# Norms, logits and choice of experts of a routed FFN, made block by block inside the attention stream before it

## The chip, the cores and the metric

The kernel runs on one core of one Trainium2 chip. The metric is the device time of the whole kernel in microseconds (us): the median over runs, lower is better. The time before is 7800.91 us, the median of three runs (7788.05 to 7835.12).

The engines are named as in the profile: PE is TensorE (PEld its weight loads), DVE is VectorE, ACT is ScalarE, POOL is GpSimd, SP is SyncE, which here only issues DMAs. Each runs its own queue in order, and semaphores tie the queues together.

## The reference, cut to what matters

Four layers run over 6250 nodes of 256 numbers. Every edge list has 206,250 edges, in order of their target node. The change touches the first two layers:

```python
x = x + _L0_gnn_ref(_layernorm(x), edge_index, ...)      # attention over the edges
x = x + _L0_ffn_ref(_layernorm(x)[None], ...)[0]         # routed FFN, 8 experts, top 2
x = x + _L1_gnn_ref(_layernorm(x), src, dst, edge_weight, ...)
x = x + _L1_ffn_ref(_layernorm(x)[None], ...)[0]

def _L0_ffn_ref(x, Wr, br, ln_g, ln_b, W1, b1, W2, b2):  # N = 6250, D = 256, E = 8, H = 1024
    xt = x.reshape(N, D)
    logits = xt @ Wr + br
    probs = softmax(logits)
    top_p, top_idx = top_k(probs, 2)
    weights = top_p / top_p.sum(-1, keepdims=True)
    xn = (xt - mean(xt)) * rsqrt(var(xt) + 1e-5)
    xe = xn[None] * ln_g[:, None] + ln_b[:, None]        # for each expert
    h = gelu(xe @ W1 + b1);  y = h @ W2 + b2
    return (weights[:, :, None] * y at top_idx).sum(1)
```

So the FFN's input is normed once (xt, which the router reads) and once more without weights (xn, which the experts read).

## The kernel before, in words

X, the nodes' state, stays in SBUF as 49 blocks of 128 nodes. The inputs are sorted on the chip in other places of the program; here the path `fast()` runs, which the kernel takes when the edges are in order of their targets.

**The first attention's stream** (`gat_stream`, called for `s0`). First come the edge rows (L1792 on), then the projection (L1809 to 1838), which writes one row of 260 numbers for each node to a table in DRAM (`tab`) and keeps each node's two parts of the score in `NI`. `gat_stream` splits these into three bfloat16 parts, `NB` (L1170 to 1175), and stores them to DRAM (L1177); `NB` lies in a pool that lives as long as the stream.

The edges are cut into 1612 tiles of 128 and 202 pieces of 8 tiles. For each tile, POOL gathers 128 rows of `tab` with an indirect DMA (L1214) into one of nine buffers `g`. Four pieces make a batch (51 of them). The order of the work on each engine is written out by hand (`manual_schedule`): one step of the loop issues the gathers of piece s, loads for piece s+2 on SP's queue (`db`, the targets, L1198; `nbw`, the nodes' parts, L1203; `kf`, L1207), the scores of piece s-2 (`z`, L1246, from `g` and one-hot matmuls), moves of finished sums, and the sums of piece s-7 (L1316). Once in four steps, a batch turns its scores (L1260), takes the greatest of each node by scans, turns them back, and ACT takes exponentials (L1281, L1285); DVE scales the gathered rows into messages (L1293). When the last tile of a group of nodes is summed, ACT copies the sum (`kept`, L1329, three buffers), PE shifts it into blocks (`bacc`, L1342), and `done` (L1845 to 1861) ends block b: it divides by the softmax's sum, adds the bias, takes the relu and adds to X (L1861). At the end of each part of a step `beside()` is called, which here does nothing.

**The routed FFN's head** (`ffn0`, L652 to 690) follows. For seven blocks at a time, `layernorm` (L247 to 257: statistics L252 and L253, a root on ACT at L242, a reciprocal L244, a subtract-and-scale L256) gives `xt` and, from it, `xn`. SP stores `xn` to the DRAM table `tab_x` (L671). Each block of `xt` is transposed on PE (L263), copied by ACT (L264), multiplied with Wr (L678), and DVE adds br into `lo` (L679). Then for all 49 blocks at once come softmax, `top2` (each of 392 numbers ranked against the 7 others of its node: L270 to L278), and the weights of the two chosen (`gates`, L290).

**The experts** (`routed_ffn`, L457 to 632). It loads b1, ln_g and ln_b with the biases along the partitions (L481, three DMAs, then DVE copies at L482 and a store to `par_d` at L483). The routing counts each expert's nodes with scans (L486), gives every choice a place (L491 to L538), and turns places into row numbers with 98 pairs of one-hots and a matmul (L549, L551, L553). Then 56 tiles of 256 rows: SP loads the expert's weights, POOL gathers the rows from `tab_x` (L577), PE turns them (L586), DVE scales them into `xe` (L589), and PE makes two matmul layers (L601, L614) with ACT's Gelu between (L604); POOL scatters the result (L617). After each tile four pieces of other work are issued from a generator, `beside`.

That other work is a sort of the second edge list (`sorted_edges`, L1405 on; its compares at L1447 and L1448 on DVE), then the preparation of the later streams' runs. The generator's work carries no dependence on the FFN's head. Outside the stream a scheduler orders the instructions, and it puts the sort's first operations into DVE's queue from the end of the stream on.

After that come the second GNN layer (POOL gathers at L234, weighted sums at L1921) and a second attention stream whose gathers are again at L1214.

Of the kernel before, what the change touches and what calls it, by code (L numbers as in the profile page):

```python
# [20 lines left out]
F32 = mybir.dt.float32  # L21
BF = mybir.dt.bfloat16
I32 = mybir.dt.int32
I16 = mybir.dt.int16
AF = mybir.ActivationFunctionType
# [7 lines left out]
P = 128  # L33
# [38 lines left out]
def tile_kernel(ctx, tc, src_ins, out):  # L72
# [192 lines left out]

    def top2(pool, v, n_exp, nt=NT):
# [3 lines left out]
        nc.vector.memset(rank, 0.0)  # L270
        for j in range(n_exp):
            for a, b, op in ((0, j, OP.is_gt), (j + 1, n_exp, OP.is_ge)):
                if a < b:
                    nc.vector.tensor_tensor(cmp[:, :, a:b], v[:, :, j:j + 1].to_broadcast([P, nt, b - a]),
                                            v[:, :, a:b], op=op)
                    nc.vector.tensor_add(rank[:, :, a:b], rank[:, :, a:b], cmp[:, :, a:b])
# [4 lines left out]
    def per_row(pool, op, a, n_exp, name):  # L281
        r = pool.tile([P, NT], F32, name=name)
        nc.vector.tensor_reduce(r, a, AX.X, op)
        return r[:, :, None].to_broadcast([P, NT, n_exp])

    def divide(pool, dst, a, by, n_exp, name):
        r = pool.tile([P, NT], F32, name=name)
        nc.vector.tensor_reduce(r, by, AX.X, OP.add)
        nc.vector.reciprocal(r, r)
        nc.vector.tensor_mul(dst, a, r[:, :, None].to_broadcast([P, NT, n_exp]))  # L290
# [166 lines left out]
    def routed_ffn(keep, tab_x, sel, gates, pre, beside):  # L457
# [12 lines left out]
        par_d = dram.tile([n_exp, P, NPAR], F32, name="par_d")  # L470
# [4 lines left out]
        with tc.tile_pool(name="rk", bufs=1) as p, tc.tile_pool(name="rkw", bufs=4) as wp, \  # L475
                tc.tile_pool(name="rk_ps", bufs=1, space=PSUM) as pp:
            par = p.tile([P, n_exp, NPAR], F32, name="par")
            with nc.allow_non_contiguous_dma(reason="biases along the partitions"):
                for o, n, v in ((0, FC, b1), (FC, KD, I[f"{pre}_ln_g"]), (FC + KD, KD, I[f"{pre}_ln_b"])):
                    pt = p.tile([P, n_exp, n], F32, name=f"par{o}")  # L480
                    nc.sync.dma_start(pt, v.rearrange("e (c p) -> p e c", p=P))  # L481
                    nc.vector.tensor_copy(par[:, :, o:o + n], pt)  # L482
                nc.sync.dma_start(par_d.rearrange("e p c -> p e c"), par)  # L483
# [168 lines left out]
    def ffn0(beside):  # L652

        E0 = I["L0_ffn_Wr"].shape[1]
        with tc.tile_pool(name="f0", bufs=1) as f0:
            gates = f0.tile([P, NT, E0], F32, name="gates")
# [1461 lines left out]
```

## Time and profile before

| | us |
|---|---|
| median of three runs | 7800.91 (7788.05 to 7835.12) |
| the profiled execution's own time | 6605.39 |
| its span | 6603.6 |
| first gather of the first stream | 173.8 |
| last gather of the first stream ends | 2206.7 |
| last block of X is written | 2251.1 |
| `gates` are written | 2396.6 |
| first one-hot of the routing | 2418.2 |
| first matmul of the experts | 2476.3 |
| experts end | about 3324 |

Busy in the whole span: PE 3864.8, PEld 2941.4, DVE 4398.8, ACT 1008.9, POOL 4097.0 us. The profiled execution is one run, 1195 us shorter than the median of the timed runs; the profile's page doesn't say why. The mean granted TensorE clock of that execution is 0.75.

How to read the profile's lines: a group gives source line, engine, operation, out<-in with the tiles' names and shapes, the count, then the busy time in us, the mean of one in ns, and the idle time of the engine just before, with what ended most of it. A line of the timeline gives start and length in us and, in brackets, the idle time before and what released it; "SPq" is a DMA issued by SP. A line of the waits gives the engine, what it was about to do, whom it waited for, and us in total, times and the longest. In the page's 40 slices (165 us each) POOL is busy 7 tenths in slices 2 to 13 and 2 to 3 tenths in slices 14 to 20; PE is at 9 tenths in slices 16 to 19:

```profile
PE   4466666666666659999913566666666667111111
DVE  5455555555555683345267888888888883888888
ACT  2000000000000102222300122222222223000000
POOL 0777777777777302233217777777777775777774
```

### The profile page before, as it was taken

Reading aid. Unit: us, or ns where it says so; the run is one execution under the profiler, and the core shown is the slowest. Engines: PE = TensorE matmul, PEld = TensorE weight load, DVE = VectorE, ACT = ScalarE, POOL = GpSimd, SP = SyncE. Lnnn points to the kernel's source line nnn. Section 1 sums busy time; section 2 is a strip of 40 time slices with the busy share of each in tenths; the row PEclk is TensorE's granted clock in tenths of the full one; section 3 lists DMA queues with packets and bytes.
Section 4 is the critical chain, followed back from the end, with each engine's and each line's share of the span. In section 5 each row is a group of like instructions: output and inputs, shape, how many; then the busy total and the mean of one; then the engine's idle time right before and its main releaser. Section 6 shows DMA issues by size and latency. Waiting matters only on the chain.

```text
span 6603.6 us, 62175 instructions
## 1 busy us (share of the span) xinstructions
PE 3864.8 (59%) x17463; PEld 2941.4 (45%) x17463; DVE 4398.8 (67%) x10540; ACT 1008.9 (15%) x2527; POOL 4097.0 (62%) x4320
## 2 busy tenths in 40 slices
PE   4466666666666659999913566666666667111111
PEld 3344444444444448888712344444444445111111
DVE  5455555555555683345267888888888883888888
ACT  2000000000000102222300122222222223000000
POOL 0777777777777302233217777777777775777774
PEclk9677777777777669999955777787888788555555
DMA  4544454554555216556553444444444443222322
GB/s 134 140 139 137 138 140 138 138 139 137 138 139 138 72 45 210 184 191 218 181 188 107 115 118 123 122 122 118 123 122 122 118 122 75 61 68 69 68 68 53
DMA packets 495558, 821.80 MB, mean 124 GB/s; under 512 B 142672, under 2 KB 314915, under 8 KB 495170
## 3 DMA queue, kind: packets, MB, share of 16 engines
q0 software_dynamic: 190880, 462.26, 26.3%
q1 hardware_dynamic: 291654, 343.79, 17.0%
q10 hardware_dynamic: 12668, 11.68, 0.6%
q8 instruction: 141, 2.31, 0.1%
q14 instruction: 215, 1.76, 0.1%
HBM read 743.27 MB, written 77.29 MB: 124 GB/s over the span
## 4 chain that ended last, share of the span: by engine, by line
POOL 33%; PE 17%; issue 17%; DVE 16%; DMA 16%; ACT 1%; DVEq 0%; ACTq 0%; SPq 0%; another core or an unknown queue 0%; POOLq 0%
POOL g L234 17%; POOL g L1214 16%; DMA g<-tab,si 7%; PE ph L601 5%; PE py L614 5%; DMA g<-tab_ef,si 3%; PE acc L1316 3%; DMA g<-tab_1f,si1s 2%; DVE run L1921 2%; DVE X L1756 2%; DVE g L1293 1%; DVE oh L1107 1%; PE ph L1830 1%; DVE ot L1224 1%; DVE z L1246 1%
## 5 line engine op out<-in xcount | busy, mean ns | idle before, releaser
L234 POOL DMA_INDIRECT g<-tab_ef,si x1616 | 1533.1, 949 | 601.7 <-issue 574.3
L1214 POOL DMA_INDIRECT g<-tab,si x1612 | 1539.6, 955 | 493.7 <-issue 411.2
L1921 DVE SCALAR_TENSOR_TENSOR run<-g,wab,run 128x256 f32<-128x256 f32 x2626 | 1264.5, 488 | 337.7 <-DMA g<-tab_ef,si 261.3
L1316 PE MATMUL acc<-g,oh 128*128 128x264 f32 x3224 | 1054.0, 493 | 338.4 <-DVE g L1293 333.4
L1316 PEld LDWEIGHTS acc<-g,oh 128*128 128x128 f32 x3224 | 780.7, 250 | 561.7 <-DVE g L1293 392.0
L1214 POOL DMA_INDIRECT g<-tab_1f,si1s x787 | 770.1, 979 | 251.5 <-issue 212.5
L2035 PE MATMUL acc<-run,oh 128*128 128x256 f32 x808 | 320.8, 537 | 707.7 <-DVE oh L1925 707.0
L2035 PEld LDWEIGHTS acc<-run,oh 128*128 128x128 f32 x808 | 199.6, 264 | 817.6 <-issue 431.2
L1246 DVE TENSOR_TENSOR z<-g,nd 128x32 f32<-128x32 f32 (+1 forms) x301 | 58.1, 193 | 717.5 <-DMA g<-tab,si 654.8
L1293 DVE TENSOR_TENSOR g<-g,pe 128x2048 f32<-128x2048 f32 (+2 forms) x301 | 487.4, 1619 | 0.0
L1657 PE MATMUL pf<-xt,w 128*128 128x512 f32 (+1 forms) x832 | 419.0, 639 | 105.9 <-ACT h L1662 99.1
L1316 PE MATMUL acc<-s,oh 128*128 128x72 bf16 x1267 | 96.7, 251 | 593.6 <-DVE s L1298 593.6
L1668 PE MATMUL pf<-w,h 128*128 128x256 f32 x1568 | 400.2, 405 | 68.2 <-ACT y L1673 56.9
L601 PE MATMUL ph<-xe,w 128*128 128x256 f32 x1792 | 404.1, 382 | 4.3 <-DVE xe L589 4.3
L614 PE MATMUL py<-w,h 128*128 128x256 f32 x1792 | 398.6, 380 | 0.0
L577 POOL DMA_INDIRECT xg<-tab_x,gi x112 | 123.7, 1105 | 403.6 <-PE pt L586 317.9
L1668 PEld LDWEIGHTS pf<-w,h 128*128 128x128 f32 x1568 | 314.3, 205 | 128.6 <-ACT y L1673 64.5
L601 PEld LDWEIGHTS ph<-xe,w 128*128 128x128 f32 x1792 | 340.9, 192 | 49.8 <-DVE xe L589 4.7
L1316 PEld LDWEIGHTS <-oh 128*128 128x128 bf16 x1267 | 90.4, 134 | 597.5 <-issue 494.1
L614 PEld LDWEIGHTS py<-w,h 128*128 128x128 f32 x1792 | 336.5, 191 | 42.9
L617 POOL DMA_INDIRECT tab_y<-y,so x112 | 119.0, 1063 | 275.3 <-DVE y L616 270.8
L1235 PEld LDWEIGHTS <-ot 128*128 128x128 bf16 x2879 | 116.1, 101 | 388.2 <-DVE ot L1224 347.2
(494 smaller groups left out, 5764.0 us busy)
## 6 DMA issues: line engine op xcount, KB each, us to landing
w<-in_L_ffn_W SPq DMA_DIRECT2D x112, 1024.0 KB
db<-s_d SPq DMA_DIRECT2D x299, 256.0 KB
g<-tab_ef,si POOLq DMA_INDIRECT x1616
g<-tab,si POOLq DMA_INDIRECT x1612
y_d<-y SPq DMA_DIRECT2D x196, 128.0 KB
yb<-y_d SPq DMA_DIRECT2D x49, 512.0 KB
g<-tab_1f,si1s POOLq DMA_INDIRECT x787
yy<-tab_y SPq DMA_DIRECT2D x7, 1792.0 KB
```

The costliest lines, as they stand in the source:

```text
L234: nc.gpsimd.indirect_dma_start(out=dst, out_offset=None, in_=table, in_offset=bass.IndirectOffsetOnAxis(ap=si[:, t:t + 1], axis=0))
L601: nc.tensor.matmul(ph, w1[:, k, f * P:(f + 1) * P], xe[:, k, :], start=(k == 0), stop=(k == KD - 1))
L614: nc.tensor.matmul(py, hs[f][:, i * P:(i + 1) * P], w2[:, f, :], start=(f == 0), stop=(f == FC - 1))
L1214: nc.gpsimd.indirect_dma_start(out=g[:, j, :DH + H], out_offset=None, in_=tab, in_offset=bass.IndirectOffsetOnAxis(ap=si[:, t0 + j:t0 + j ...
L1246: nc.vector.tensor_add(z[:, :n], g[:, :n, DH:DH + H], nd[:, :n, :H])
L1293: nc.vector.tensor_mul(gh, gh, ps[i][:, o:o + n, :, None].to_broadcast([P, n, H, CD]))
L1316: nc.tensor.matmul(acc[b].rearrange("p s w -> p (s w)"), oh[:, t - a], m_, start=(t == lo), stop=(t == hi))
L1657: nc.tensor.matmul(ph[:, :n], w1[:, e, k, f * P:(f + 1) * P], xts[g][:, k, :n], start=(k == 0), stop=(k == KD - 1))
L1668: nc.tensor.matmul(py[:, :D], hs[g, e, f][:, j * P:(j + 1) * P], w2[:, e, f, :], start=(f == 0), stop=(f == FC - 1))
L1756: nc.vector.scalar_tensor_tensor(X[:, b, :], v[:, e, :], gates[:, j, e:e + 1], X[:, b, :], op0=OP.mult, op1=OP.add)
L1921: nc.vector.scalar_tensor_tensor(at[:, i] if j < Q - 1 else r[i], g[:, j, :], w, at[:, i], op0=OP.mult, op1=OP.add)
L2035: nc.tensor.matmul(acc[i], oh[:, k], r[k], start=(q % 2 == 0 and k == 0), stop=(last and k == 1))
```

## The change

The head of the FFN moves into the stream. A class `Head` holds `lo`, `sel`, `gates`, `wr`, `br` and the two DRAM tables; it is made before the edge rows are loaded, so the loads of `wr` and `br` stand first on SP's queue. The bias loads become a generator (`expert_params`), of which a step runs at each `beside()` of the stream: the three loads at its first step, the copies and the store 20 steps later.

Every ending of a block now goes on over the following steps of the stream, one part in each: `done` returns `normed`, that returns `twice`, that `logits`. Each adds statistics and a root of one block (`spread`) or a reciprocal and a scaling (`scaled`); `twice` makes the transposes, `logits` writes the block's row to `tab_x` (49 stores of 128 KB where there were seven of seven blocks) and the logits, which ACT copies from PSUM. After blocks 21, 43 and 48 the choice of experts is made for the blocks since the last choice (22, 22 and 5), one part in each step (`select`, `ranks`).

Around it: the exponentials `pe`, the transposes and the logits share one PSUM tile (`mix`), `il` becomes bfloat16 (it holds 0 and 1), `kept` has two buffers for three, and `NB` moves from the stream's own pool into the pool `split`, which is closed before the pools `gw` (with the gathers' buffers) and `gp` are opened.

In the order of instructions that is built, the sort's compares of the second edge list no longer lie ahead of the first expert; tiles 2 to 5 of the experts hold 20 each.

```diff
@@ routed_ffn
-            par = p.tile([P, n_exp, NPAR], F32, name="par")
-            with nc.allow_non_contiguous_dma(reason="biases along the partitions"):
-                for o, n, v in ((0, FC, b1), (FC, KD, I[f"{pre}_ln_g"]), (FC + KD, KD, I[f"{pre}_ln_b"])):
-                    pt = p.tile([P, n_exp, n], F32, name=f"par{o}")
-                    nc.sync.dma_start(pt, v.rearrange("e (c p) -> p e c", p=P))
-                    nc.vector.tensor_copy(par[:, :, o:o + n], pt)
-                nc.sync.dma_start(par_d.rearrange("e p c -> p e c"), par)
@@ new functions
+    def ranks(rank, cmp, v, n_exp):
+
+        nc.vector.memset(rank, 0.0)
+        for j in range(n_exp):
+            for a, b, op in ((0, j, OP.is_gt), (j + 1, n_exp, OP.is_ge)):
+                if a < b:
+                    nc.vector.tensor_tensor(cmp[:, :, a:b], v[:, :, j:j + 1].to_broadcast([P, rank.shape[1], b - a]),
+                                            v[:, :, a:b], op=op)
+                    nc.vector.tensor_add(rank[:, :, a:b], rank[:, :, a:b], cmp[:, :, a:b])
+            yield
+    def select(pool, tag, lo, br, sel, gates, n, n_exp):
+
+        wide = [P, n, n_exp]
+        nc.vector.tensor_add(lo, lo, br[:, None, :].to_broadcast(wide))
+        nc.vector.tensor_sub(lo, lo, per_row(pool, OP.max, lo, n, n_exp, f"mx{tag}"))
+        nc.scalar.activation(lo, lo, AF.Exp)
+        yield
+        divide(pool, gates, lo, lo, n, n_exp, f"sm{tag}")
+        yield
+        yield from ranks(sel, lo, gates, n_exp)
+        nc.vector.tensor_scalar(sel, sel, 1.5, None, op0=OP.is_lt)
+        nc.vector.tensor_mul(gates, gates, sel)
+        divide(pool, gates, gates, gates, n, n_exp, f"sg{tag}")
@@ gat_stream
-            mp = pool("gw", 2)
-            pp = pool("gp", 1, space=PSUM)
             nid = window_nodes(s, gp)
-            NB = gp.tile([P, NT, 3, ND], BF, name="NB")
             nb_d = dram.tile([NP, 3 * ND], BF, name=f"{s.name}_nb") if s.group else None
             nbw, sums_of, ready, moved = {}, {}, [], []
             with tc.tile_pool(name="split", bufs=1) as sp:
+                NB = (sp if s.group else gp).tile([P, NT, 3, ND], BF, name="NB")
...
                 if s.group:
                     nc.sync.dma_start(nb_d.rearrange("(t p) d -> p t d", p=P), NB.rearrange("p t s d -> p t (s d)"))
+            mp = pool("gw", 2)
+            pp = pool("gp", 1, space=PSUM)
...
-                for s_ in range(max(npiece + 7, PB * nbatch + 3) + 2):
+                last, s_, later = max(npiece + 7, PB * nbatch + 3) + 1, -1, []
...
+                while s_ < last or later:
+                    s_ += 1
                     if s_ < npiece:
                         gathers(s_)
                     if s_ + 2 < npiece:
                         load(s_ + 2)
                     beside()
+                    now, later[:] = list(later), []
+                    for f, a in now:
+                        follow(f(*a))
...
-                            done(b, sums_of.pop(b), items.pop(b), mp)
+                            follow(done(b, sums_of.pop(b), items.pop(b), mp))
@@ first attention's stream
+                return normed, (b, mp) + spread(mp, X[:, b, :])
+            def spread(mp, x):
+                bs = mp.tile([P, 6], F32, name="bs", bufs=3)
+                nc.vector.bn_stats(bs, x)
+                mv = mp.tile([P, 2], F32, name="mv", bufs=6)
+                nc.vector.bn_aggr(mv, bs)
+                sd = mp.tile([P, 1], F32, name="sd", bufs=6)
+                nc.scalar.activation(sd, mv[:, 1:2], AF.Sqrt, bias=eps)
+                return mv, sd
+            def scaled(mp, xl, x, mv, sd):
+                rs = mp.tile([P, 1], F32, name="rs")
+                nc.vector.reciprocal(rs, sd)
+                nc.vector.tensor_scalar(xl, x, mv[:, 0:1], rs, op0=OP.subtract, op1=OP.mult)
+            def normed(b, mp, mv, sd):
+                xt = mp.tile([P, D], F32, name="xt", bufs=3)
+                scaled(mp, xt, X[:, b, :], mv, sd)
+                return twice, (b, mp, xt) + spread(mp, xt)
+            def twice(b, mp, xt, mv, sd):
+                pt = mix[:, P:P + D].rearrange("p (k e) -> p k e", k=KD)
+                for k in range(KD):
+                    nc.tensor.transpose(pt[:, k], xt[:, k * P:(k + 1) * P], ident)
+                xT = mp.tile([P, KD, P], F32, name="xT")
+                nc.scalar.copy(xT, pt)
+                return logits, (b, mp, xt, mv, sd, xT)
+            def logits(b, mp, xt, mv, sd, xT):
+                scaled(mp, xt, xt, mv, sd)
+                nc.sync.dma_start(head.tab_x[b * P:(b + 1) * P], xt)
+                head.logits(mix[:, P + D:P + D + E0], xT, b)
+                if b in ends:
+                    t0 = max([e + 1 for e in ends if e < b], default=0)
+                    return chosen, (head.select(hp, t0, b + 1 - t0),)
+            ends = (NT // 2 - 3, NT - 6, NT - 1)
...
-            gat_stream(s0, H0, C0, si, il, dl, tab, NI, early, done)
+                par = head.params(hp)
+                gat_stream(s0, H0, C0, si, il, dl, tab, NI, early, done, beside=lambda: next(par, True) is None,
+                           pe=mix[:, :P].rearrange("p (b h) -> p b h", h=H0))
```

## The prediction

> **What bounds the kernel now.** I read four views, in this order. First the busy times of the engines in seven stretches of the span, from the first gather of the first attention's stream to the end of the routed FFN. The columns are stretch, length, then PE, PE's weight loads, DVE, ACT and POOL busy, granted clock, DMA share, GB/s.
> ```profile
> 173.00:2206.00 2033.00, 1250.82 (x5369) 932.47 (x5370) 1145.57 (x2071) 109.31 (x489) 1539.31 (x1616) 0.75 0.51 138
> 2251.00:2397.00 146.00, 66.99 (x294) 58.65 (x294) 122.60 (x461) 24.83 (x66) 4.86 (x57) 0.50 0.15 52
> 2397.00:2418.00 21.00, 1.00 (x4) 0.93 (x4) 14.96 (x48) 0.00 (x0) 0.40 (x3) 0.50 0.36 5
> 2476.00:3324.00 848.00, 828.81 (x3989) 724.03 (x3989) 313.04 (x572) 245.25 (x495) 234.88 (x219) 0.99 0.59 192
> ```
> The stream (row one) is set by POOL; DVE is 56% busy there, ACT 5%. The next 146 us hold the norms, logits and choice of experts, with DVE 84% busy and POOL and PE nearly idle; then 21 us of routing; the experts at the end fill PE. So 167 us stand between two stages that other engines bound.
>
> The page's groups and the waits from 300 to 2100 us say why POOL sets the stream:
> ```profile
> L1214 POOL DMA_INDIRECT g<-tab,si x1612 | 1539.6, 955 | 493.7 <-issue 411.2
> ```
> ```profile
> DVE z L1246 <- DMA g<-tab,si: 565.8, 134, 5.9
> ```
> A gather costs 0.955 us and 0.30 us to the next: 1612 x 1.255 = 2023 of the 2033 us. DVE stands 566 us waiting for what POOL gathers, so DVE work added there is free until these 566 us are full, if it doesn't touch POOL. Between last sum and first expert, the timeline has:
> ```profile
> 2250.66 0.43 DVE L1861 SCALAR_TENSOR_TENSOR X<-o,X 128x256 f32<-128x256 f32 x1
> 2254.74 1.28 ACT L242 ACT_TABLE_LOAD   x1 [6.20 <-DVE sign L1417]
> 2256.03 0.30 ACT L242 ACTIVATE sd<-mv,eps 128x7 f32<-128x7 f32 x1
> 2396.07 0.56 DVE L290 TENSOR_TENSOR gates<-pb,sg 128x392 f32<-128x392 f32 x1
> 2404.96 0.20 DVE L482 COPY par<-par 128x64 f32<-128x64 f32 x1 [5.16 <-DMA par<-in_L_ffn_b]
> 2418.17 0.28 DVE L549 TENSOR_SCALAR ro<-iota,r 128x128 f32<-128x128 f32 x1
> ```
> The last X is done at 2251.1; the routing's first one-hot starts at 2418.2.
>
> **What is removed.** 2418.2 - 2251.1 = 167.1 us. These groups of 2251 to 2397 us carry the cost of what moves (busy us, mean ns):
> ```profile
> L678 PE MATMUL pr<-wr,xT 128*128 128x8 f32 x196 | 43.2, 347 | 0.6
> L263 PE MATMUL pt<-ident,xt 128*128 128x128 f32 x98 | 31.3, 438 | 58.2 <-DVE xt L256 45.4 <-issue 10.8 <-ACT xT L264 1.5
> L264 ACT COPY xT<-pt 128x256 f32<-128x256 f32 x49 | 18.2, 372 | 54.2 <-PE pt L263 31.1 <-PE pr L678 22.7
> L252 DVE BATCH_NORM_STATS2 bs<-X 128x6 f32<-128x256 f32 x49 | 18.2, 409 | 0.0
> L256 DVE TENSOR_SCALAR xt<-X,mv,rs 128x256 f32<-128x256 f32 x49 | 16.4, 410 | 0.0
> L253 DVE BATCH_NORM_AGGREGATE mv<-bs 128x2 f32<-128x6 f32 x98 | 16.2, 171 | 0.0
> L1447 DVE TENSOR_TENSOR A<-A 128x512 f32<-128x512 f32 x17 | 11.6, 682 | 0.0
> L1448 DVE TENSOR_TENSOR A<-A 128x512 f32<-128x512 f32 x16 | 10.7, 666 | 0.0
> ```
>
> **What comes in its place after the last sum.** Only the last block still has its endings there, and the last five their choice. By rows: statistics 0.41 + 0.17; a table load and sd 1.28 + 0.30; reciprocal 0.19 and scaling 0.41, the second statistics 0.58 (1.2); two transposes, a copy, four logits matmuls and a copy about 2.3; add, greatest, subtract 0.5; table load and Exp 1.6; the softmax's division 0.65; 14 compares and 14 adds on 5x8 numbers at 169 to 198 ns (the rank rows on 12 numbers) 5.1; threshold, product and division 0.9. With about 1 us of handovers: 15 us. The routing's 21 us stay but for two things: the wait for the biases (5.16 + 0.43 + 0.44 = 6 us, since their loads go to the stream's start) and some 7 to 9 sort compares of 0.67 that the scheduler had put between (5 to 6 us). In the built order, ten wide conversions of the sort remain ahead of the first expert, about 4 us of them in this part: 14 us. So 167 becomes 29: **a gain of 138**.
>
> **What the stream takes in.** Per block DVE gets two statistics, two aggregates, two reciprocals and two scalings: 2 x (0.41 + 0.17 + 0.19 + 0.41) = 2.36 us, 116 us over 49 blocks, and three selections of some 12 us: 152 us beside 566 us of waiting, at nothing. Without that cover they would cost 152. PE gets 31.3 + 43.2 = 75 us of transposes and logits in a stage where it is busy 1251 of 2033: nothing. ACT gets copies (49 x 0.5), 100 roots at 0.30, and Sqrt alternating with the stream's Exp: about 100 table loads at 1.28 = 128 us on an engine 5% busy. They sit ahead of the messages' Exp (L1281) and the copies of finished sums (L1329), for which DVE and then PE wait; what they delay are chains that POOL doesn't wait for while its nine buffers, about 20 us of gathers, are not full. Nothing, therefore, but see the third rival. SP gets 49 stores of 128 KB instead of seven of 896 KB, each waiting for its scaling, with the next pieces' loads (db, nbw, kf) queued behind it. Those are issued two steps of 10 us early, so a store that is one scaling late (2 us) takes nothing from the pieces. The loads of Wr and br now stand ahead of the edge rows' load: two issues of 0.4, **1 us**.
>
> Three things are not free. (a) NB now lies in a pool that is closed before the stream's buffers open, so the first gather's buffer may use its space, and in the built order the first gather waits for NB's store. Before:
> ```profile
> 173.82 1.10 POOL L1214 DMA_INDIRECT g<-tab,si  x1 [0.45 <-POOL s_nid L1137]
> 175.65 0.36 SPq L1177 DMA_DIRECT2D s_nb<-NB  x1
> 188.53 0.33 SPq L1203 DMA_DIRECT2D nbw<-s_nb  x1
> ```
> The store's 6,272 pieces of 48 bytes are issued at 175.65, and nbw, which reads them, goes out at 188.53. So gathers start between 177 (store instantly done) and 188.5 instead of 173.8: 3 to 15, taken at **13**, since nbw's queue has nothing else to wait for. (b) The tail: POOL's last gather ends at 2206.7 and the last X at 2251.1; one step for each ending makes batches end a little later; **3** (0 to 10). (c) The ports. POOL issues the gathers, and DVE's operations may hold it up. In the stream's 1612 gathers, what exceeds 0.945 us sums to about 21 us, over 1146 us of DVE work; 155 more give 21 x 155/1146 = **3 to 4**.
>
> Here the Trainium skill speaks against the change: "SBUF — State Buffer", section "Who interferes with whom", says a tensor_scalar can run in a mode that takes the port pair which DVE shares with GpSimd, and that the loser fully blocks for the whole instruction. By that, 98 scalings x 0.41 = 40 us of POOL instead of 4, and the gain falls by 36. In the trace the same scaling op (L1995) of a later stream, 0.49 us long, meets a lengthened gather only 14 of 49 times, 0.9 us in all. I take the row; 40 is the range's end. A second rule: "ScalarE: Activation LUTs", section "What ACT_TABLE_LOAD costs", puts a switch at 2.66 us with the drain; here the root starts at 2256.03, as the load of 2254.74 ends: 1.28. By the page ACT would get 271 us instead of 131, still inside its idle 1900.
>
> **What comes back later.** The sort of the second stream filled DVE's gaps in the 167 us: 33 compares of 0.67 (L1447, L1448) and about ten in the routing. Of some 51 before the first expert none is left there, so 34 us of DVE work move into the experts' tiles, where DVE is busy 313 of 848. In the built order tiles 2 to 5 hold 20 compares each, 13.3 + 1.9 of own DVE work = 15.2 against PE's 14.35 a tile: 0.8 a tile, 3 to 4 us, inside the turned rows' lead of some 5 us. From the sixth tile both orders are alike. **0 to 1**, and 35 if nothing covers it.
>
> **Sum.** -138 + 13 + 3 + 4 + 1 + 0 = -117. The profiled execution took 6605.39 us (span 6603.6), so 6488 profiled. The median is 7800.91, 1195 us above; nothing in the page says where these lie, and I leave the gain in us unscaled: **7684**.
>
> **Rivals.** *A, the gain grows with the timed runs' length.* If the 1195 us are spread evenly (7800.9/6605.4 = 1.181), 117 becomes 138: 7663. For it: the granted clock of 0.75 leaves room, and PE's stages may stretch. Against: this section is DVE's and the gathers POOL's, and neither shows a clock.
>
> *B, part is taken back.* The full lock: -117 + 36 = -81, 7720; or the sort's 35 us return on the experts' path: 7719; both: 7755. For it: the page's rule, and 20 compares in a tile leave DVE full. Against: L1995's row, and 535 us of DVE idle among the experts.
>
> *C, slower: table loads pace the stream.* Sqrt and Exp alternate in every batch; if POOL had to wait for each load, 102 x 1.28 = 131 of cost against 117 of gain: +14, 7815; with 2.66, +154, 7955. It decides from 117/102 = 1.15 us reaching POOL for each load. For it: L1246's z and the messages are one chain over DVE, ACT and PE. Against: POOL's idle time is issue, 0.30 each, and it runs nine pieces ahead.
>
> *D, the change does nothing:* the scheduler could leave the endings behind the stream. The built order has them between the batches: no chance given.
>
> **How the numbers follow.** Forecast 62%, own range 7660 to 7705 (the NB wait 3 to 15, tail 0 to 10, ports 0 to 10, the sort's 0 to 4). A 13%, B 17% (7705 to 7790), C 8%. The three runs of before lie within 0.6%. The range 7635 to 7770 takes in A and most of B. One per cent, about what this measurement can tell, is 7723 and 7879: faster 62 + 13 and a little of B, 77%; same most of B, 15%; slower C, 8%.
>
> **What would show it.** Right: gathers 1.25 us apart, DVE still waiting for gathers (some 400 us); the first gather at 186 to 188; last X to first one-hot 27 to 33 us; the wait for the biases gone; experts about 848 us with PE full. Wrong: POOL waiting for a release in the stream (C), lengthened gathers beside the scalings (B), PE waiting for DVE's xe in the first tiles (B), or a profile down by 117 and a median that isn't.

## The result and the profile after

| | before | after |
|---|---|---|
| median, 11 runs each | 7814.48 us (7780.39 to 7835.12) | 7779.05 us (7751.27 to 7796.53) |
| ratio | | 0.996, 95% interval 0.9944 to 0.9977 |

The change saves 0.4%, some 35 us where 117 were predicted: within 1%, outside the range, and faster all the same. In later series (kernels timed together) before's median moved between 7805 and 7895 us, so ratios are compared only inside one series; copies of after gave 0.9952 (0.9933 to 0.997) and 0.9913 (0.9889 to 0.9938).

After's profiled execution has a span of 7781.5 us, the pace of the timed runs. The page of before, on which the prediction rests, has 6603.6. A copy of before was therefore profiled again (e0_before below): span 7799.2. It is the one to set beside after.

The stretches of after, with the columns of the prediction's first fence: stream, endings that are left, routing, experts.
```profile
190.00:2640.00 2450.00, 1224.78 (x5591) 944.24 (x5592) 1265.32 (x2480) 272.93 (x761) 1539.55 (x1612) 0.71 0.44 117
2701.00:2714.00 13.00, 1.68 (x6) 1.21 (x6) 9.38 (x58) 2.58 (x7) 1.54 (x4) 0.50 0.06 20
2714.00:2728.00 14.00, 0.99 (x4) 0.93 (x4) 13.02 (x47) 0.00 (x0) 3.72 (x54) 0.50 0.27 76
2785.00:3629.00 844.00, 828.18 (x3990) 722.88 (x3990) 347.71 (x628) 245.67 (x495) 238.47 (x221) 0.99 0.58 193
```
The same of the second profile of before:
```profile
175.00:2530.00 2355.00, 1167.17 (x5319) 887.12 (x5320) 1151.71 (x2056) 110.61 (x486) 1536.61 (x1612) 0.73 0.45 119
2583.00:2729.00 146.00, 66.98 (x294) 58.65 (x294) 122.56 (x461) 24.82 (x66) 5.00 (x57) 0.50 0.15 52
2729.00:2750.00 21.00, 0.99 (x4) 0.93 (x4) 14.93 (x48) 0.00 (x0) 0.26 (x2) 0.50 0.35 5
2808.00:3657.00 849.00, 830.72 (x3989) 725.21 (x3989) 312.74 (x572) 245.24 (x495) 235.76 (x219) 0.99 0.59 191
```
The 146 us became 13, the 21 became 14, the experts kept their length. But the stream, 2033 us on the page, lasts 2355 in before and 2450 in after, with the same 1612 gathers and the same 1540 us of POOL work. POOL's row of after's page, and three places of its timeline:
```profile
L1260 POOL DMA_INDIRECT g<-tab,si x1612 | 1539.6, 955 | 924.5 <-issue 577.4
```
```profile
190.09 1.11 POOL L1260 DMA_INDIRECT g<-tab,si  x1 [14.66 <-DMA s_nb<-NB]
...
993.27 0.51 PE L702 MATMUL mix<-wr,xT 128*128 128x8 f32 x4
993.64 0.35 PE L1281 MATMUL pd<-nbw,ot 128*128 128x24 bf16 x8
1000.67 0.17 ACT L703 COPY lo<-mix 128x8 f32<-128x8 f32 x1 [12.09 <-remote]
...
1012.57 0.36 DVE L1290 TENSOR_REDUCE nd<-pd 128x64 f32<-128x192 f32 x1 [19.98 <-remote]
1019.05 0.95 POOL L1260 DMA_INDIRECT g<-tab,si  x1 [6.83 <-PE pd L1281]
...
2700.78 0.43 DVE L1921 SCALAR_TENSOR_TENSOR X<-o,X 128x256 f32<-128x256 f32 x1
2713.84 0.18 DVE L296 TENSOR_TENSOR gates<-gates,sg 128x40 f32<-128x40 f32 x1
2728.38 0.28 DVE L578 TENSOR_SCALAR ro<-iota,r 128x128 f32<-128x128 f32 x1
```
A gather still takes 955 ns, but POOL's idle time before gathers is 924.5 us (493.7 on the page). The first line is the wait for NB's store that was predicted; the last three are the short section after the stream. Between them is what nobody reckoned with: the matmuls of `pd` (the nodes' parts of a piece's scores) are recorded at 993.64, DVE is idle, and yet the reduction that reads them, `nd`, starts at 1012.57, nearly 20 us later; the logits' copy, too, comes 7 us after its matmuls. The release that `nd` waits for is a count of PE's semaphore; "remote" means that no instruction is recorded to end where that count came. At 1019.05 POOL has stopped 6.83 us for want of a buffer.

**The balance**, from timelines (us; the page in the first column):

| | page of before | before again | after | after less before again |
|---|---|---|---|---|
| first gather starts | 173.8 | 175.4 | 190.1 | +14.7 |
| first to last gather | 2032.8 | 2354.3 | 2449.4 | +95.1 |
| last gather to last X | 44.4 | 53.1 | 61.7 | +8.6 |
| last X to `gates` | 145.6 | 145.6 | 12.8 | |
| `gates` to first one-hot | 21.6 | 21.6 | 14.4 | -140.0 with the row above |
| experts | 848 | 848.9 | 844.5 | -4.4 |
| POOL's stops over 0.5 us in the stream | 1, of 2 us | 120, of 363 us | 112, of 453 us | |
| start of `nd` after the recorded end of its matmuls, where DVE stood idle before it (300 to 2400 us), mean (sum) | 0.05 (under 1) | 5.1 (604) | 6.0 (697) | |

Of the 95.1 us that the gathers take longer, 90 are longer stops of POOL. The rows sum to -26.0; the other stages add about 8 (the gathers of L234, which the change doesn't touch, take 15.0 more, those of the second attention 6.4 less), so the spans differ by -17.7; the medians differ by 35 (the interval is 18 to 44). The 1195 us between page and timed runs lie in the gather stages: this stream +321, the gathers of L234 +383 (2025.1 to 2408.1), the second attention's +413.5 (1009.7 to 1423.2).

### The profile page after: what moved, and what is told of

It is laid out like the page before. It is cut to its first block, busy times and chain, and to the rows that moved or that the text cites. A ratio compares the mean times of both kernels' runs of the same rounds, so it can differ in the third digit from the quotient of the medians.

```text
span 7781.5 us, 62325 instructions
## 1 busy us (share of the span) xinstructions
PE 3827.1 (49%) x17463; PEld 2901.2 (37%) x17463; DVE 4464.9 (57%) x10655; ACT 1161.1 (15%) x2758; POOL 4096.1 (53%) x4320
## 5 line engine op out<-in xcount | busy, mean ns | idle before, releaser
L234 POOL DMA_INDIRECT g<-tab_ef,si x1616 | 1537.3, 951 | 995.4 <-issue 557.9
L1260 POOL DMA_INDIRECT g<-tab,si x1612 | 1539.6, 955 | 924.5 <-issue 577.4
L1363 PE MATMUL acc<-g,oh 128*128 128x264 f32 x3224 | 981.8, 465 | 174.6 <-issue 105.7
L1363 PEld LDWEIGHTS acc<-g,oh 128*128 128x128 f32 x3224 | 747.6, 238 | 365.0 <-issue 127.7
L1290 DVE TENSOR_REDUCE nd<-pd 128x64 f32<-128x192 f32 (+1 forms) x301 | 105.8, 352 | 1138.1 <-remote 914.2
L1714 PE MATMUL pf<-xt,w 128*128 128x512 f32 (+1 forms) x832 | 479.7, 715 | 474.9 <-issue 163.3
L2142 PE MATMUL acc<-run,oh 128*128 128x256 f32 x808 | 295.2, 500 | 628.3 <-DVE oh L2032 261.6
L1340 DVE TENSOR_TENSOR g<-g,mix 128x2048 f32<-128x2048 f32 x202 | 457.5, 2265 | 0.0
L1714 PEld LDWEIGHTS pf<-xt,w 128*128 128x128 f32 x832 | 179.7, 235 | 665.2 <-issue 321.6
L1306 PE MATMUL zt<-ident,Z 128*128 128x128 f32 x228 | 76.6, 400 | 676.7 <-issue 380.2
```

The lines of the kernel that those rows point to most:

```text
L234: nc.gpsimd.indirect_dma_start(out=dst, out_offset=None, in_=table, in_offset=bass.IndirectOffsetOnAxis(ap=si[:, t:t + 1], axis=0))
L1260: nc.gpsimd.indirect_dma_start(out=g[:, j, :DH + H], out_offset=None, in_=tab, in_offset=bass.IndirectOffsetOnAxis(ap=si[:, t0 + j:t0 + j ...
L1340: nc.vector.tensor_mul(gh, gh, ps[0][:, o:o + n, :, None].to_broadcast([P, n, H, CD]))
L1363: nc.tensor.matmul(acc[b].rearrange("p s w -> p (s w)"), oh[:, t - a], m_, start=(t == lo), stop=(t == hi))
L1714: nc.tensor.matmul(ph[:, :n], w1[:, e, k, f * P:(f + 1) * P], xts[g][:, k, :n], start=(k == 0), stop=(k == KD - 1))
L2142: nc.tensor.matmul(acc[i], oh[:, k], r[k], start=(q % 2 == 0 and k == 0), stop=(last and k == 1))
```

## The experiments

Each line gives the median, the ratio to before in its own series with its interval, and from the trace the time from first to last gather ("gathers") or from the first `nd` to the last X. `...` stands where a diff is cut.

**e0_before: before, profiled again.** No edit.

> The kernel before, unchanged, for a profile that belongs to a run of about 7800 us; the one on the page took 6605. Theory 1 (the stream is not POOL's in such a run): POOL stops before the first gather of many pieces for want of a free buffer, the stream takes 2300 to 2400 us instead of 2033, and PE's signals come later than its recorded ends. Theory 2 (the stream is POOL's here too, and the after kernel alone slows it): gathers 1.25 us apart, the stream 2033 us, and the 1195 us lie in later stages. Either way the experts' 848 us and the 146 us of norms should be as on the page within 5 us.

7801.06 us, span 7799.2. Its timeline has what after's has:
```profile
1033.08 0.35 PE L1235 MATMUL pd<-nbw,ot 128*128 128x24 bf16 x8
...
1041.48 0.36 DVE L1244 TENSOR_REDUCE nd<-pd 128x64 f32<-128x192 f32 x1 [5.31 <-remote]
...
1041.99 1.05 POOL L1214 DMA_INDIRECT g<-tab,si  x1 [3.14 <-ACT kept L1329]
```
So before already runs with PE's results late by 5 us in the mean and with POOL stopping 120 times; the page's execution had neither. The gather stages set both kernels' time, but not at POOL's own 1.255 us a gather.

**Which part of the endings costs? One part out at a time (one series).** e1_no_pe: no transposes, logits and their copies. e2_no_root: the roots made adds. e3_no_rows: the rows written once, ahead of the stream.
```diff
e1 -                for k in range(KD): nc.tensor.transpose(pt[:, k], ...)
e1 -                nc.scalar.copy(xT, pt)
e1 -                head.logits(mix[:, P + D:P + D + E0], xT, b)
e2 -                nc.scalar.activation(sd, mv[:, 1:2], AF.Sqrt, bias=eps)
e2 +                nc.vector.tensor_scalar(sd, mv[:, 1:2], 1e-5, None, op0=OP.add)
e3 -                nc.sync.dma_start(head.tab_x[b * P:(b + 1) * P], xt)
e3 +                nc.sync.dma_start(head.tab_x.rearrange("(t p) d -> p t d", p=P), X)   # ahead of the stream
```


> The kernel after without the endings' transposes, logits and their two copies on ACT (the logits stay zero, so every node goes to the first two experts); norms, roots, rows and choice stay. Theory P (in the measured runs PE paces the stream, and each PE instruction that is added to its queue lengthens it): the stream's 2449 us fall by 70 to 100 to about 2355, the time to about 7690. Theory A (the table loads pace it): at most 20 us. Theory S (row stores delay the next pieces' loads): none. Theory D (DVE's added work paces it): at most 20.

> The kernel after with the endings' root on ACT replaced by an addition on DVE: no Sqrt, so about 98 table loads fewer (126 us of ACT) and 98 activations fewer; 98 DVE operations of about 0.1 us more. The values of the norms are not the reference's. Theory A: the stream falls by 70 to 100 us, the time to about 7690. Theory P: at most 20, as ACT's loads only shift what PE waits for. Theories S and D: none.

> The kernel after without the 49 row stores in the stream; the table of rows is written once before it from the nodes' state, so its content is not the reference's. Theory S: the stream falls by 50 to 95 us. Theories P, A and D: within 15 us.

e1 7797.45, 0.9896 (0.9875 to 0.9918), gathers 2402.7. e2 7800.22, 0.9901 (0.987 to 0.9932), 2399.2. e3 7811.79, 0.9908 (0.9886 to 0.993), 2425.8. Before was 7894.55 here. The series had no copy of after. Beside after's ratio of 0.9913 in the series most like it (e12, before 7884.9) none gains more than 0.2%; beside 0.9952 (e5) each would gain about 0.5%. No one part is thereby shown to be the cost, and none is cleared to better than some 40 us.

**e4_half_sums: is it the amount of PE's work?** Before with every second tile's sum matmul left out.
```diff
-                        if (t - t0 < 2) == (part == 0):
+                        if (t - t0 < 2) == (part == 0) and (parts > 1 or t % 2 == 0 or t in (lo, hi)):
```


> The kernel before with every second tile's sum on PE left out in the first attention's stream (half the messages are not summed), all else the same. Theory P: the stream of 2354 us goes to POOL's own pace, 2040 to 2100, and the time falls by 250 to 310 to about 7520. If DVE or ACT pace it: less than 60 us, stops of POOL stay over 250 us in sum.

7860.0, 0.9956 (0.9943 to 0.9969), gathers 2350.5; 97 stops of POOL, 349 us. Half of these matmuls are worth 0.4%: PE's amount of work is not the pace. `nd` even comes 9.8 us late in the mean.

**e5_after and e8_no_endings: what do the endings cost in all?** e8 keeps the change's other edits (two `kept`, NB's pool, the shared PSUM tile, the early loads) but makes no endings in the stream; after it come one store of X as rows and, in the source, one choice on zero logits. That choice waits for nothing in the stream, and in the trace it runs at the stream's start (`gates` at 210.7).
```diff
-                return normed, (b, mp) + spread(mp, X[:, b, :])
...
+                nc.sync.dma_start(head.tab_x.rearrange("(t p) d -> p t d", p=P), X)
+                for _ in head.select(hp, 0, NT):
+                    pass
```


> The kernel after, unchanged, as the neighbour of the three others on the same chip: about 35 us under the kernel before, the stream's gathers about 95 us longer than before's 2354, the stretch from the last X to the first one-hot about 27 us.

> The kernel after without any of the endings' continuation in the stream: no norms, transposes, logits or rows there (the rows are the nodes' state, stored after the stream, the logits are zero, and one choice for all blocks is made after it). What stays are the moved loads, the pool of NB, two buffers for kept and the shared PSUM tile. If the continuations make all of the stream's 95 us: the gathers take 2354 plus or minus 20 from first to last. If the other edits (two kept buffers above all) have a part: that part stays on top.

e5 7765.11, 0.9952 (0.9933 to 0.997), gathers 2438.1. e8 7684.65, 0.9841 (0.9814 to 0.9869), gathers 2360.2, as in before (2354). The endings thus cost **80 us** by the medians, 13.5 of them what is left behind the stream (last X to first one-hot 27.2 in e5, 13.7 in e8), so some 67 in the stream; the two profiles put last X 90 us apart (2687.7 and 2598.1). The other edits cost nothing in the stream. With a section of 13.7 left of 167.2, and the first gather later by 14, the prediction's working gives e8 about 139 of gain; 7809 - 7685 = 124 was measured (0.9841; the interval is 102 to 145 us). The removal is worth what was predicted, within that interval.

**e6_after_own and e7_before_own: do the sum matmuls wait for too many releases?** The messages go to a tile of their own, so that these matmuls wait for DVE alone and ACT once a piece; the gathers keep seven buffers.
```diff
-                g = piece[q] = mp.tile([P, Q, W], F32, name="g", bufs=9)
+                g = piece[q] = mp.tile([P, Q, W], F32, name="g", bufs=7 if parts == 1 else 9)
...
+                m = mp.tile([P, Q, W], F32, name="m", bufs=2) if parts == 1 else g
+                nc.vector.tensor_mul(mh, gh, ...)
+                    nc.scalar.copy(m[:, :n, DH:], g[:, :n, DH:])
```


> The kernel after, with the messages written to a tile of their own (two buffers, gathers' buffers 9 to 7) instead of over the gathered rows, and one small copy on ACT for each piece. PE's sums then wait for DVE and ACT once a piece, where each of the eight matmuls waited for a gather's semaphore. Theory W (PE is late because each of its matmuls waits on a gather's semaphore, though the rows landed long ago): PE's signals come on time, the stream falls from 2449 to 2040 to 2120, the time to about 7450. Theory R (PE's signals are late in these runs whatever it waits for): the stream stays within 60 us of 2449.

> The same edit on the kernel before. Theory W: the stream falls from 2354 to 2035 to 2100, the time by 250 to 320. Theory R: within 60 us of before. Under W the after kernel with this edit is about 110 to 130 us faster than this one, as the endings then lie beside POOL's gathers; under R only some 20 to 60.

e6 7968.57, 1.0214 (1.018 to 1.0249), gathers 2623.6; e7 8104.01, 1.0395 (1.0347 to 1.0443), gathers 2618.1, `nd` 11.0 us late. The lateness is not a matter of how many releases the matmul waits for; with fewer buffers it only costs more. The pair shows something else: with this edit the kernel after is 135 us faster than the kernel before, where 20 to 60 was expected if PE stays late, and the two spend the same time on gathers (5.5 us apart) and in POOL's stops (630 and 625 us). Here, where a gather's buffer no longer waits for the sums, the endings cost next to nothing in the gathers' time, and most of the removal is left.

**e10_before_g10: does a longer lead cover it?** A tenth buffer, room made by `il` in bfloat16.
```diff
-                g = piece[q] = mp.tile([P, Q, W], F32, name="g", bufs=9)
+                g = piece[q] = mp.tile([P, Q, W], F32, name="g", bufs=10 if parts == 1 else 9)
```


> The kernel before with ten gather buffers in the first stream instead of nine (the flags il in bfloat16 make the room), nothing else. Theory L (POOL's lead over the other engines is what late signals use up, so the buffers set the stream's time): the stream's 2354 falls by 80 to 200, the stops of POOL from 363 us to under 250. If an engine's own throughput sets it: within 20 us.

7885.57, 1.001 (0.9995 to 1.0025), gathers 2369.5, 128 stops, 378 us in all. No: a tenth buffer is no use.

**e9_grouped and e11_after_ln: the table loads (rival C), one series.** e9 makes the roots for groups of 8, 8, 8, 8, 8, 5, 2, 1 and 1 blocks. e11 makes the root by Ln and Exp, which doubles the switches.
```diff
e9  -                nc.scalar.activation(sd, mv[:, 1:2], AF.Sqrt, bias=eps)
e9  +                nc.scalar.activation(sd[:, :, :n], v[:, :, :n], AF.Sqrt, bias=eps)   # n up to 8
e11 -                nc.scalar.activation(sd, mv[:, 1:2], AF.Sqrt, bias=eps)
e11 +                nc.scalar.activation(sd, mv[:, 1:2], AF.Ln, bias=eps)
e11 +                nc.scalar.activation(rs, sd, AF.Exp, scale=-0.5)
```


> The kernel after with the endings' roots taken for groups of blocks (8, 8, 8, 8, 8, 5, 2, 1, 1) in one activation, first and second norm together: the second norm's variance is worked out from the first (var/(var+eps), mean 0), so the second statistics go; scaling, transposes, logits and rows follow one block a step. About 18 table loads instead of 98, 49 x 0.58 us of DVE fewer. If what is taken back is the sum of the instructions that stand in the chain over ACT, DVE and PE (theory C), the stream's 2440 falls by 35 to 60 and the last X to first one-hot stays near 28: time about 7715 where the kernel after has 7765 and before 7809. If only PE's part counts: within 15 of the kernel after.

> The kernel after with each root made as a logarithm and an exponential on ACT: the built order then has four table loads for each block instead of two, about 98 more (126 us of ACT), 98 more small activations, and 98 reciprocals fewer on DVE. Theory C: the stream grows by 35 to 60 us, the time to about 7815. If table loads are hidden: within 15 us of the kernel after.

e9's loads, of its groups:
```profile
L1950 ACT ACT_TABLE_LOAD x9 | 11.5, 1283 | 0.2
...
L1328 ACT ACT_TABLE_LOAD x8 | 10.3, 1283 | 64.7 <-remote 40.4 <-PE zt L1323 10.3 <-PE zt L1324 9.0
```
and e11's:
```profile
L1931 ACT ACT_TABLE_LOAD x98 | 125.7, 1283 | 1.7
L1933 ACT ACT_TABLE_LOAD x98 | 125.7, 1283 | 1.7
```
17 loads: 7800.3, 0.9904 (0.9877 to 0.9931), gathers 2409.3. 196 loads: 7804.0, 0.9913 (0.9885 to 0.9942), gathers 2414.6. Some 180 loads, 230 us of ACT, move the time by 4 us, inside both intervals, where C's working charges 1.28 us for each load. The two also differ in DVE's work (e9 has no second statistics, e11 no reciprocals), which by e14 below doesn't set the time. Rival C is refuted.

**e12_after, e13_dve_only, e14_no_dve: the endings in two halves, one series.** e13 keeps only DVE's half (no transposes, logits or rows in the stream, and an add on DVE for each root), e14 only the other half (no statistics and scalings; one choice after the stream).
```diff
e13 -                nc.scalar.activation(sd, mv[:, 1:2], AF.Sqrt, bias=eps)
e13 -                    nc.tensor.transpose(...); nc.scalar.copy(xT, pt); head.logits(...); nc.sync.dma_start(head.tab_x[...], xt)
e14 -                nc.vector.bn_stats(bs, x); nc.vector.bn_aggr(mv, bs)
e14 -                nc.vector.reciprocal(rs, sd); nc.vector.tensor_scalar(xl, x, ...)
```


> The kernel after, unchanged, once more, since the times of before drift by up to 1% from one series to the next (7809 to 7895) and only kernels of one series can be compared: about 40 us under before in a series where before is near 7810, and, if the late kernels of the slow series are no guide, 70 to 90 under it where before is near 7880.

> The kernel after with only DVE's part of the endings left in the stream: statistics, reciprocals, scalings and choice stay; no transposes, logits or copies (logits zero), no roots on ACT (an addition on DVE in their place), no row stores (the table is written once before the stream). Values are not the reference's. Theory D (DVE's added work stands in the stream's chain from DVE over PE back to DVE, at about its own length): within 25 us of the kernel after of this series. If PE, ACT or the rows make the 80 us that all continuations cost together: 50 to 80 us faster than after.

> The reverse: the endings' transposes, logits, copies, roots with their table loads and row stores stay, on the nodes' state and a constant variance; no statistics, reciprocals or scalings, and one choice for all blocks after the stream. Values are not the reference's. Theory D: 50 to 80 us faster than the kernel after. If PE, ACT or rows make the cost: within 25 us of it. Parts that share it would put both kernels between.

e12 7813.07, 0.9913 (0.9889 to 0.9938), gathers 2426.7. e13 7759.18, 0.9831 (0.9809 to 0.9853), gathers 2388.5. e14 7833.34, 0.993 (0.9903 to 0.9957), gathers 2437.4; its choice after the stream explains 6 of the 20 us over e12. Without PE's, ACT's and SP's part the time falls by 54 us, to the ratio that e8 has without endings; without DVE's part it doesn't fall. DVE's added 114 us of work are thus not what costs; the steps on PE, ACT and SP are, taken together.

The traces show by which way. In after, e5, e8, e12, e13 and e14, as in e0, the gathers without POOL's stops take 1991 to 2000 us; what differs is the stops (363 us in e0, 366 in e8, 396 in e13, 427 to 453 in the four that keep PE's and ACT's part). And the stops end elsewhere. From after's waits and its timeline (L703 is ACT's copy of the logits):
```profile
POOL g L1260 <- ACT lo L703: 131.0, 31, 6.7
```
```profile
488.26 0.17 ACT L703 COPY lo<-mix 128x8 f32<-128x8 f32 x1 [6.70 <-PE mix L702]
488.62 0.94 POOL L1260 DMA_INDIRECT g<-tab,si  x1 [5.98 <-ACT lo L703]
```
and from e13's waits, of the same 300 to 2400 us:
```profile
POOL g L1261 <- ACT g L1333: 92.3, 24, 5.2
```
POOL stops for a count of ACT's semaphore that comes with the logits' copy, and ACT has waited for PE's logits before it. Over the whole stream after has 32 such stops, e5, e12 and e14 have 33 to 36. In e13 and e8, without these copies, the stops end with ACT's writes to `g` and with `kept`, as in e0, so far as an end is named (42 of after's 112 have none).

**e15_one_load, e16_eight_loads, e17_after_one: no gathers by POOL.** e15: before, each piece's eight gathers replaced by one load of 1024 consecutive rows on SP. e16: by eight loads. e17: after with one load. The rows are other rows than the reference's.
```diff
e15 e17 +  nc.sync.dma_start(g[:, :n, :DH + H], tab[r:r + n * P].rearrange("(t p) d -> p t d", p=P)); return
e16     +  for j in range(n): nc.sync.dma_start(g[:, j, :DH + H], tab[r':r' + P])
```


> The kernel before with each piece's eight gathers on POOL replaced by one plain load of 1024 consecutive rows by SP: the same bytes into the same buffers, no POOL in the stream, an eighth of the landings; the rows are not those of the edges. If PE's late signals come with the gathers (their landings, or POOL's work): nd starts within 0.5 us of pd's recorded end, and the stream runs at the chain of DVE and PE, 1600 to 2000 us from first load to last X instead of 2407. If PE is late of itself: 2250 or more.

> The kernel before with each of the stream's gathers replaced by a plain load of 128 consecutive rows by SP: as many transfers and landings as the gathers have, the same bytes into the same buffers, but no POOL; the rows are not those of the edges. If the number of landings holds PE up: nd starts 3 us or more after pd's recorded end and the first nd to the last X takes 2000 us or more. If it is POOL's making of the gathers: nd within 0.5 us, and 1370 to 1600 us, as with one load for a piece.

> The kernel after with one plain load by SP for a piece's eight gathers, as was done to the kernel before: no POOL in the stream; the rows are not those of the edges. PE's signals should be on time here too. The stream is then the chain of DVE and PE at about 6.8 us a step, 5.8 of them DVE's, so nothing covers the endings: if DVE's length counts, first nd to last X is 100 to 160 us longer than the 1368 of before with one load, and the kernel after is then faster than before by the 140 less these: 0 to 45 us. If the endings fit into PE's and DVE's gaps: less than 60 longer, and 80 or more faster.

| | median | ratio | first `nd` to last X | `nd` late, mean |
|---|---|---|---|---|
| before again (e0) | 7801.06 | | 2388.7 | 5.1 us |
| e15 | 6827.15 | 0.8653 (0.8632 to 0.8674) | 1368.3 | 0.05 us |
| e16 | 6803.16 | 0.872 (0.8691 to 0.8748) | 1382.4 | 0.05 us |
| e17 | 6921.88 | 0.886 (0.8833 to 0.8887) | 1641.2 | 0.05 us |

Two lines of e16's timeline, to set beside those of e0:
```profile
1000.87 0.35 PE L1240 MATMUL pd<-nbw,ot 128*128 128x24 bf16 x8
1001.26 0.36 DVE L1249 TENSOR_REDUCE nd<-pd 128x64 f32<-128x192 f32 x1
```
The stretches of the stream in e16:
```profile
187.00:1569.00 1382.00, 1078.54 (x5483) 853.52 (x5483) 1173.58 (x2113) 113.03 (x504) 0.00 (x0) 0.88 0.70 203
```
and in e17:
```profile
191.00:1832.00 1641.00, 1166.47 (x5777) 920.26 (x5773) 1297.71 (x2578) 286.74 (x794) 0.00 (x0) 0.84 0.58 174
```
In e16 the reduction starts 0.04 us after the matmuls' end. As many landings, more DMA (203 GB/s for 119), but no work on POOL: PE is on time and the stream 1000 us shorter (e15's, too, is below the 1600 to 2000 us expected). So neither the number of landings nor the amount of DMA makes PE late, but something that comes with POOL's gathers alone: POOL's work on them, the DMA queue of their own that they use, or the scattered rows they read. No run separates these three, and they don't suffice by themselves: the page's execution of before has them all and no lateness.

In e17, where neither POOL nor a late PE covers them, the endings lengthen the stream by 273 us over that of e15, which has the same loads (by 259 over e16's); DVE is busy 1298 of 1641 there. The kernel is 119 us slower than e16, of its own series: 259 less the 140 gained. The 100 to 160 us expected were too few. That endings spread over many steps in order have a price of their own, once nothing else is waited for, is a reading that no run tests.

## Why the prediction was wrong

**Right in mechanism and size.** *What is removed, and what comes in its place*: 138 predicted, 140 measured, 15 and 14 us for the two parts that stay, 12.8 and 14.4 found. *NB's store*: the first gather 13 us later, 14.7 found. *The tail*: 3 (0 to 10), 8.6 found, near the range's end. *The ports*: the row won over the rule of "SBUF — State Buffer" that the prediction weighed against it: 98 scalings more, and a gather's mean is 955 ns on the page and in after (953 in e0), where 40 us would have made it 980. The rule says that such an operation can take the ports; whether these did, no run shows. *What comes back later*: 0 to 1, and the experts went from 848.9 to 844.5. Two small terms were misreckoned without weight: 21 x 155/1146 is 2.8, not 3 to 4, and a tile of the experts takes PE 14.7 us on the page, not 14.35.

**The step that failed** is "What the stream takes in", and ahead of it "The stream (row one) is set by POOL". The step put DVE's 152 us (114 came), PE's 75 and ACT's table loads in "at nothing", because the chains are ones "that POOL doesn't wait for while its nine buffers, about 20 us of gathers, are not full". That is true of the page's execution: one stop over 0.5 us. In the pace of the timed runs PE's results reach `nd` 5 to 6 us late in the mean and up to 24, at the first link of the chain from `pd` to the messages and the finished sums; no buffer is free about 120 times, and POOL waits for that chain. An ending puts transposes, logits, copies and roots into the queues of the engines that this chain runs over. e13 shows that it is this half that costs, and the traces that its cost is POOL's stops: 453 us for 363, of which 31 stops, 131 us, end with the logits' copy on ACT, which had waited for PE. Where the buffers come free without the sums (e6 and e7), the endings add 5 us to the gathers. Priced at nothing, the step cost 95 us in the two profiles and some 67 by the medians of e5 and e8. 117 - 67 = 50 to 117 - 95 = 22; 35 was measured, with 18 to 44 as the interval.

**Where it could have been seen.** The prediction says of the 1195 us: "nothing in the page says where these lie, and I leave the gain in us unscaled". An execution 1195 us shorter than the median is not the one that is timed. The page could not price the missing time, but it could not carry a step "at nothing" either: the covers (POOL's pace, nine buffers of lead) were read from an execution without such stops. The 152 us that the prediction itself names as the price without cover belonged into the range, which ended at 7770; as a bound only, for by e13 and e14 it is not DVE's work that was paid for.

**The rivals.** *A* fell: the removed section is 167 us in both profiles of before; what stretches is the gathers' stages. *B* fell in both halves (955 ns; experts not longer), although 7779 lies inside its 7705 to 7790; that is luck. *C* was nearest in sort, a chain over DVE, ACT and PE that POOL waits for, and wrong in its cause: between 17 and 196 loads there is no difference beyond the intervals.

**What stays open.** Why PE's results come late while gathers are under way, and why the page's execution of before was free of it. The traces of the timed pace also hold only about one in six of the gathers' landing events (2.2 for each us, 12.6 on the page), so that waits for landings can be followed only in part. Which of the transposes, roots and rows carries how much of the 54 us isn't settled either: e1 to e3 lacked a copy of after in their series.

## What to carry to other kernels

Set the profiled execution's own time beside the median first; where they differ by 15%, profile again, and find the stages that differ before any wait is called covered. Work moved into a stage with a spare engine is free only if it isn't a link in a chain whose buffers run empty: count the stops of the engine that is said to set the pace, not its busy share. Price such work by leaving it out of the finished kernel (e8), one run that separates what is removed from what is taken in.

## What the runs showed of the hardware

**PE's results can come long after its matmuls are recorded.** `nd` is late by 5.1 us in e0 and 0.05 in e15 and e16, where POOL makes no gathers. In e0's stream the gaps over 0.6 us between the counts of PE's semaphore sum to 2012 us, and some 1240 of these lie in gaps within 0.04 us of a multiple of 0.70; on the page of before the common gaps are 0.44 and 0.88 us, in e0's experts 0.43 and 0.86. The granted clock doesn't explain it: 0.75 in the page's stream, 0.73 in e0's. After's own trace holds both kinds. While gathers go on without a stop, 371 of 771 gaps over 0.38 us lie at multiples of 0.70 and 214 at 0.44 or 0.88; once POOL has stood still for 3 us (in its 30 stops over 4.5 us), 5 of 106 and 90. So in this pace PE is slow while gathers are under way and recovers when they pause.

The Trainium skill, "SBUF — State Buffer", section "Who interferes with whom", gives PE and ACT ports of their own and names the pair of DVE and GpSimd as the only source of contention in that memory. Whether this lateness arises in that memory at all, no run here shows.

**A table load costs 1.283 us and nothing around it shows:** e11's 196 loads have 3.4 us of idle time of ACT before them in all, and doubling them left the gathers' time as it was (2414.6 us; 2426.7 to 2449.4 in the kernel after and its copies).
